# Output scatters of the last layer, issued behind the gathers of a later slot

## The chip, the cores and the metric

One core of one Trainium2 chip runs the whole computation in one launch. The metric is the device time of that launch in microseconds (us). Before the change three runs gave 2300.34, 2286.70 and 2286.37 us; the median is 2286.7 us.

## The reference

Sixteen graphs share one adjacency of 1024 nodes (about 8 edges in a row of 1024), with 128 features for each node. Four layers follow each other: three graph transformers (L0, L2, L3) and one graph attention layer (L1). The last one, L3, is what the change touches:

```python
Q, K, V = (h @ Wq), (h @ Wk), (h @ Wv)          # 8 heads of 16
scores = where(adj == 0, -inf, Q K^T / sqrt(16))
attn_out = softmax(scores) @ V
x = layer_norm(h + attn_out @ Wo + bo)
x = layer_norm(x + relu(x @ W1 + b1) @ W2 + b2)
```

The returned array holds x of L3 for every graph and node.

## The kernel before

**The sparse way.** Only the edges are computed. Nodes are sorted by degree and handled in blocks of 128 destinations. For each layer a table in DRAM holds one row of keys and values for each node; for a group of 8 graphs a row of an attention layer has 2048 floats (8 KB). A block's edges are packed in chunks: a chunk is 128 edge slots, one for each partition, and one indirect DMA on POOL's queue (`gathered`, L942) fetches the 128 table rows of a chunk, 1 MB if no slot is empty.

**Units, parts, slots.** A unit is one block of one group in one layer (2 groups of 8 blocks in each layer, 64 units). A unit's chunks are taken two at a time, and one more chunk (called MIX) is taken alone; each of these is a part. Most units have five parts, in the order pair, pair, pair, MIX, pair; block 0 has six and block 7 four. I call them p0, p1, p2, MIX, p3. The loop of the schedule (L1152) makes one pass for each part; a pass is a slot. In slot i VectorE (DVE) multiplies the gathered keys by the queries (`products`, L954), sums over a head (`exponentials`, L977), and weights the values of the part before (`weighted(i - 1)`, L1005). ScalarE (ACT) takes the exponent between these two; TensorE (PE) adds the weighted rows to their destinations (L1021).

**Gathers.** There are four buffers `e` (`EDGES = 4`). When `weighted(i - 1)` has read its buffer, L1195 refills it: `gathered(i - 1 + AHEAD)` with `AHEAD = 4`, so that slot i fetches the part of slot i + 3. In a five-part unit slot 0 fetches this unit's MIX, slot 1 its p3, and slots 2, 3 and 4 fetch p0, p1 and p2 of the next unit.

**Tails.** When a unit's sums are complete, `divided` (L1058, L1061) divides them in slot 1 of the next unit and leaves two tails (`attention_tail`), one for each half h of the group's 8 graphs. A tail is a generator of 13 steps: output projection, layer norm, feed-forward, layer norm, and in the last layer `finish` (L655), which turns the result back into rows (`outs`), yields twice and sends them to the output with an indirect scatter on POOL's queue (L676): 128 rows of 2 KB, 256 KB. A pacer (`others`, L1095) spreads 11 steps over the following slots. What is left is run at once when the next `divided` comes up, again in slot 1, behind that slot's gathers:

```python
                gathered(i - 1 + AHEAD)
                for _ in sizes:
                    pass
            if closing is not None and here:
                while any(gen not in free for gen in tails):
                    advance(tails)
```

With 11 paced steps out of 13, both scatters of a unit (h0 and h1) fall into this last stretch. The tile framework places the waits: an instruction that writes a tensor waits for those before it that wrote the same tensor. Each engine runs its instructions in the order in which the program issues them. The other instruction on POOL is the small sum `seen` (L1073), which `sizes` issues behind the gathers of slot 2.

So POOL's order in a five-part unit of the last layer is: MIX | p3, p3, scatter h0, scatter h1 | p0, p0, seen | p1, p1 | p2, p2, where a bar ends a slot. SyncE's queue (SP) loads the next block's features (L871) and copies a few query rows for MIX (L918).

Of the kernel before, what the change touches and what calls it, by code (L numbers as in the profile page):

```python
# [44 lines left out]
GR = 2  # L45
G = B // GR
HF = 2
# [90 lines left out]
def sparse_path(ctx: ExitStack, tc: tile.TileContext, a: dict, out: bass.AP, flag):  # L138


    nc = tc.nc
# [42 lines left out]
    places = const.tile([P, GR, HF, T], I32, name="places")  # L184
# [17 lines left out]
    def gather_buffer():  # L202
        return gathers.tile([P, max(4 * ROW, J * (ROW + G))], F32, tag="e", name="e")
# [434 lines left out]
    def turned(z, dst, gain=None, shift=None, dve=False):  # L638

        ps = bank([P, GH, P])  # L640
        for i in range(GH):
            nc.tensor.transpose(ps[:, i, :], z[:, i, :], ident)  # L642
        if dve and gain is None:
            nc.vector.tensor_copy(dst, ps)
        elif dve:
            nc.vector.tensor_scalar(dst, ps, gain, shift, ALU.mult, ALU.add)
        elif gain is None:
            nc.scalar.copy(dst, ps)  # L648
        else:
            nc.scalar.activation(dst, ps, AF.Identity, bias=shift, scale=gain)  # L650
# [4 lines left out]
    def finish(l, g, t, h, z, gain, shift, dve=False):  # L655
        if l + 1 < len(LAYERS):

            wanted[0] = True
            while held[0]:
                advance(slow)  # L660
            wanted[0] = False
            busy[0] += 1
            xn = states.tile([P, GH, P], F32, tag="xT", name="xT")
            turned(z, xn, gain, shift)
            yield "free"
            yield from project(l + 1, g, t, h, xn)
            busy[0] -= 1
            return
        xn = states.tile([P, GH, P], F32, tag="xT", name="xT")
        turned(z, xn, gain, shift, dve)  # L670
        yield
        o = twos.tile([P, GH, D], F32, tag="kv", name="outs")
        turned(xn, o, dve=dve)
        yield
        yield
        nc.gpsimd.indirect_dma_start(  # L676
            out=out.rearrange("n (k c) -> (n k) c", k=GR * HF),
            out_offset=bass.IndirectOffsetOnAxis(ap=places[:, g, h, t : t + 1], axis=0),
            in_=o.rearrange("p g d -> p (g d)"), in_offset=None,
        )  # L680

    def hidden():
        return ones_.tile([P, F * GH * P], F32, tag="f1", name="f1")
# [142 lines left out]
    units = [(l, g, t) for l in range(len(LAYERS)) for g in range(GR) for t in range(T)]  # L826
# [10 lines left out]
    def is_attention(u):  # L837
        return LAYERS[units[u][0]][1] is ATTN
# [86 lines left out]
    def gathered(i):  # L925
        if i >= len(parts):
            return
        u, pieces = parts[i]
        if u == T:
            while slow:  # L930
                while busy[0] and not held[0]:
                    advance(tails)
                advance(slow)
        l, g, t = units[u]
        width = tables[l, g].shape[1]
        many = 2 if is_attention(u) else J
        e = gather_buffer()
        es[i] = e[:, : many * width].rearrange("p (k c) -> p k c", k=many)
        for k, (j, r) in enumerate(sum(pieces, [])):
            if j == MIX:  # L940
                j, r = SHARED[t][0], COUNT[t][SHARED[t][0]]
            nc.gpsimd.indirect_dma_start(  # L942
                out=es[i][:, k, :], out_offset=None, in_=tables[l, g][:, :],
                in_offset=bass.IndirectOffsetOnAxis(
                    ap=idx[:, min(l, 1), t, j, r : r + 1], axis=0
                ),
                bounds_check=N - 1, oob_is_err=False,
            )
# [124 lines left out]
        nc.gpsimd.tensor_tensor(seen[:, :, :n], seen[:, :, :n], both, ALU.add)  # L1073

    tails = []
    fronts = []
    loads = []
    slow = []
# [3 lines left out]
    def advance(gens):  # L1082
        for gen in list(gens):
            got = next(gen, "end")
            if got == "end":
                gens.remove(gen)
            elif got == "free":
                free.append(gen)
# [23 lines left out]
    with tc.manual_schedule():  # L1112
        wide = [gather_buffer() for _ in range(EDGES)]
        setup, entry, weights = graph(wide), at_once(0), load_weights("L0")
        next(setup)
        next(weights)
        next(entry)
        more = [weights, load_graph_weights()]
        rest = slots()
        for i, room in enumerate(setup):  # L1120
            if i == T:
                for gen in more:
                    next(gen)
            if room == "load":
                for _ in loaded(0):
                    next(entry, None)
            elif room == "queries":
                for _ in entry:
                    pass
                for _ in queries(0):  # L1130
                    pass
            elif isinstance(room, str):
                next(rest)
            else:
                for _ in range(room):
                    next(entry, None)
        for _ in entry:
            pass
        scratch.close()
        prods = ctx.enter_context(tc.tile_pool(name="prods", bufs=4))  # L1140
        smalls = ctx.enter_context(tc.tile_pool(name="smalls", bufs=3))
        slow.append(at_leisure(1))
        second = loaded(1)
        next(second)
        for i in range(AHEAD - 1):
            gathered(i)
        nc.gpsimd.memset(wide[3], 0.0)
        gathered(AHEAD - 1)
        fronts.extend([islice(rest, 4), second] + more)
        closing, sizes = None, ()  # L1150
        begun = 0
        for i in range(len(parts) + 2):  # L1152
            here = i < len(parts)
            u = parts[i][0] if here else len(units)
            if here:
                l = units[u][0]
                if i and parts[i - 1][0] != u:
                    begun = i
                    if u < T - 1:
                        fronts.append(islice(rest, 4))  # L1160
                    if l + 1 < len(LAYERS) and LAYERS[l + 1][1] is ATTN:
                        if units[u][1:] == (0, 1):
                            more = load_weights(LAYERS[l + 1][0])
                            next(more)
                            next(more)
                        if units[u][1:] == (0, 4):
                            fronts.append(more)
                if is_attention(u):
                    products(i)
            if i > 1:  # L1170
                summed(i - 2)
                done = parts[i - 2][0]
                if parts[i - 1 : i] == [] or parts[i - 1][0] != done:
                    closing = divided(done)
                    next(closing)
            others()
            if here:
                exponentials(i)
            if here and i == begun + 1:
                if is_attention(u):  # L1180
                    shared(u)
                while loads:
                    advance(loads)
                if u + 1 < len(units):
                    fronts.append(queries(u + 1))
                loads.append(loaded(u + 2))
                if u:
                    advance(loads)
            others()
            if 0 < i <= len(parts):  # L1190
                weighted(i - 1, 0)
                if not is_attention(parts[i - 1][0]):
                    others()
                    weighted(i - 1, 2)
                gathered(i - 1 + AHEAD)  # L1195
                for _ in sizes:
                    pass
            if closing is not None and here:
                while any(gen not in free for gen in tails):
                    advance(tails)  # L1200
                next(closing)
                sizes, closing = closing, None
                passes = 3 if is_attention(u) else 4
                steps = STEPS if is_attention(done) else GRAPH_STEPS
                steps -= LATE[units[done][0]]
                pace[:] = 0.0, steps / (passes * sum(part[0] == u for part in parts) - 1)
            others()
            if i + 1 >= len(parts) or parts[i + 1][0] != u:

                while fronts:  # L1210
                    advance(fronts)
        while tails:
            advance(tails)
        for _ in closing:
            pass
        while tails:
            advance(tails)
# [435 lines left out]
```

## Time and profile before

The profiled execution is told by its span, from the first to the last instruction.

| | before |
|---|---|
| runs: median (lowest to highest) | 2286.7 us (2286.37 to 2300.34) |
| span of the profiled execution | 2290.8 us, 36572 instructions |
| mean granted TensorE clock | 0.956 |
| PE / DVE / ACT / POOL busy | 90% / 82% / 67% / 46% |
| gathers L942 | 576, mean 1466 ns of POOL each |
| scatters L676 | 32, median 2112 ns of POOL each, from 1735.9 to 2286.2 us |
| DMA | 636 MB, mean 278 GB/s; 59.3% of the engines' time for POOL's queue, 18.9% for SP's |

POOL's busy time is what it takes to issue a DMA; the transfer itself runs on the 16 DMA engines. A wait in POOL's queue is listed as idle time ahead of the instruction that waited, with the engine that released it; where several semaphores were waited for, the engine named is the one that came last by the records. The stretch from 1733.0 to 2224.5 us (13 units of the last layer, from one `divided` to another) is the one to look at; in it DVE is busy 417.9 of 491.5 us, PE 440.3, ACT 344.7, POOL 231.9, and the DMA engines 73%.

### The profile page before, as it was taken

Reading aid. Unit: us, or ns where it says so; the run is one execution under the profiler, and the core shown is the slowest. Engines: PE = TensorE matmul, PEld = TensorE weight load, DVE = VectorE, ACT = ScalarE, POOL = GpSimd, SP = SyncE. Lnnn points to the kernel's source line nnn. Section 1 sums busy time; section 2 is a strip of 40 time slices with the busy share of each in tenths; the row PEclk is TensorE's granted clock in tenths of the full one; section 3 lists DMA queues with packets and bytes.
Section 4 is the critical chain, followed back from the end, with each engine's and each line's share of the span. In section 5 each row is a group of like instructions: output and inputs, shape, how many; then the busy total and the mean of one; then the engine's idle time right before and its main releaser. Section 6 shows DMA issues by size and latency. Waiting matters only on the chain. (4 is left out here: it accounts for less than half of the span.)

```text
span 2290.8 us, 36572 instructions
## 1 busy us (share of the span) xinstructions
PE 2052.0 (90%) x13140; PEld 1271.6 (56%) x13140; DVE 1871.1 (82%) x1472; ACT 1530.3 (67%) x5041; POOL 1050.7 (46%) x730
## 2 busy tenths in 40 slices
PE   6479999899998999998899989999999988998987
PEld 5336666555555555554465655655655555555544
DVE  7898888588888477777988889988888887988783
ACT  3237777777776565556677777777777766776765
POOL 3355344245445278884443434333344444444540
PEclk8789999999999999999999999999999998999999
DMA  7868888678887699997998978888887877677750
GB/s 249 278 217 300 304 279 305 240 247 302 285 295 265 197 330 354 354 373 288 326 318 292 319 254 306 296 314 295 281 282 277 291 258 250 242 275 270 260 217 20
DMA packets 165197, 636.06 MB, mean 278 GB/s; under 512 B 35064, under 2 KB 37880, under 8 KB 116510
## 3 DMA queue, kind: packets, MB, share of 16 engines
q0 software_dynamic: 89216, 485.08, 59.3%
q1 hardware_dynamic: 75792, 148.57, 18.9%
q8 instruction: 105, 1.72, 0.3%
q14 instruction: 84, 0.69, 0.1%
HBM read 581.08 MB, written 92.34 MB: 294 GB/s over the span
## 5 line engine op out<-in xcount | busy, mean ns | idle before, releaser
L942 POOL DMA_INDIRECT e<-table,idx x576 | 844.2, 1466 | 1022.1 <-DVE pr L1005 796.6
L1005 DVE TENSOR_TENSOR pr<-e,ex 128x2048 f32<-128x2048 f32 (+1 forms) x320 | 661.3, 2075 | 55.9 <-ACT ex L981 32.7
L954 DVE TENSOR_TENSOR pr<-e,qr 128x2048 f32<-128x2048 f32 x192 | 439.7, 2290 | 160.3 <-DMA e<-table,idx 91.5
L1021 PE MATMUL acc<-pr,marks 128*32 128x512 f32 x2624 | 528.5, 616 | 20.3 <-DVE pr L1005 16.4
L977 DVE TENSOR_REDUCE sc<-pr 128x128 f32<-128x2048 f32 (+1 forms) x240 | 497.5, 2073 | 8.0
L620 ACT ACTIVATE z<-yps,root 128x128 f32<-128x128 f32 x888 | 319.0, 390 | 35.6 <-PE yps L735 16.8
L1021 PEld LDWEIGHTS acc<-pr,marks 128*32 128x32 f32 x2624 | 108.7, 111 | 280.9 <-issue 231.6
L635 ACT ACTIVATE z<-yps,rstd 128x128 f32<-128x128 f32 x888 | 255.0, 371 | 7.2
L731 PE MATMUL yps<-W,f 128*128 128x128 f32 x1520 | 252.6, 283 | 7.7 <-ACT f L726 1.9
L726 ACT ACTIVATE f<-ps,b 128x512 f32<-128x512 f32 x190 | 130.6, 695 | 160.4 <-PE ps L717 159.7
L731 PEld LDWEIGHTS yps<-W,f 128*128 128x128 f32 x1520 | 205.7, 193 | 51.7 <-issue 26.2
L572 PE MATMUL ps<-Wkv,xT 128*128 128x256 f32 x768 | 212.2, 417 | 20.0 <-ACT xT L648 14.4
L908 ACT COPY qr<-ps 128x512 f32<-128x512 f32 x384 | 197.1, 602 | 47.7 <-PE ps L905 47.7
L642 PE MATMUL ps<-ident,z 128*128 128x128 f32 x896 | 179.7, 300 | 41.4 <-ACT z L635 36.6
L642 PEld LDWEIGHTS ps<-ident,z 128*128 128x128 f32 x896 | 116.2, 143 | 167.7 <-ACT z L635 86.5
L717 PE MATMUL ps<-x,W 128*128 128x512 f32 x384 | 193.9, 630 | 12.5 <-ACT x L650 12.4
L620 ACT ACTIVATION_READ_ACCUMULATOR z<-yps,root 128x1 f32 x888 | 203.7, 229 | 0.0
L905 PE MATMUL ps<-q,rep 32*128 32x512 f32 x768 | 166.5, 661 | 36.4 <-ACT q L900 34.0
L572 PEld LDWEIGHTS ps<-Wkv,xT 128*128 128x128 f32 x768 | 146.5, 204 | 73.9 <-ACT qr L908 18.0
L981 ACT ACTIVATE ex<-sc 128x128 f32<-128x128 f32 (+1 forms) x240 | 76.4, 318 | 157.9 <-DVE sc L977 157.8
L576 ACT COPY kv<-ps 128x512 f32<-128x512 f32 x176 | 103.3, 593 | 108.1 <-PE ps L572 85.8
L706 PE MATMUL yps<-Wo,oT 128*128 128x128 f32 x768 | 159.9, 291 | 10.0 <-ACT oT L648 10.0
(174 smaller groups left out, 2724.2 us busy)
## 6 DMA issues: line engine op xcount, KB each, us to landing
table<-kv SPq DMA_DIRECT2D x88, 512.0 KB
kept<-xT SPq DMA_DIRECT2D x96, 256.0 KB
x<-kept SPq DMA_DIRECT2D x48, 512.0 KB
qx<-qr SPq DMA_DIRECT2D x48, 256.0 KB
e<-table,idx POOLq DMA_INDIRECT x576
table<-kv SPq DMA_DIRECT2D x32, 256.0 KB
qx<-qr SPq DMA_DIRECT2D x18, 384.0 KB
qx<-qr SPq DMA_DIRECT2D x42, 128.0 KB
```

The source lines that it names most:

```text
L572: nc.tensor.matmul(ps[:, k, :], x[:, i + k, :], w[LAYERS[l][0], "Wkv"], start=True, stop=True,)
L620: nc.scalar.activation(z[:, i, :], y[:, i, :], AF.Square, scale=D**-0.5, bias=root, accum_out=total[:, i : i + 1],)
L635: nc.scalar.activation(z[:, i, :], y[:, i, :], AF.Copy, scale=rstd[:, i : i + 1])
L642: nc.tensor.transpose(ps[:, i, :], z[:, i, :], ident)
L717: nc.tensor.matmul(ps, p["W1"][:, f * P : (f + 1) * P], x1.rearrange("p g n -> p (g n)"), start=True, stop=True,)
L731: nc.tensor.matmul(ps[:, i, :], f1[:, f, i * P : (i + 1) * P], p["W2"][:, f, :], start=(f == 0), stop=False,)
L908: nc.scalar.copy(qs[u][:, j, h * GH * D : (h + 1) * GH * D], pss[j])
L942: nc.gpsimd.indirect_dma_start(out=es[i][:, k, :], out_offset=None, in_=tables[l, g][:, :], in_offset=bass.IndirectOffsetOnAxis(ap=idx[:, ...
L954: nc.vector.tensor_tensor(prs[i][0][:, :n, :], es[i][:, :n, :ROW], qx[u].rearrange("p (o c) -> p o c", o=1) if (MIX, 0) in piece else of_p ...
L977: nc.vector.tensor_reduce(sc[:, :n, :], prs[i][0][:, :n, :].rearrange("p k (a d) -> p k a d", d=HD), mybir.AxisListType.X, ALU.add,)
L1005: nc.vector.tensor_tensor(prs[i][k0 // 2][:, :m, :].rearrange("p k (a d) -> p k a d", d=d), es[i][:, k0 : k0 + m, base : base + ROW].rearr ...
L1021: nc.tensor.matmul(outs[32 * j : 32 * j + 32], marks[:, mark, :], rhss, start=(chunk == mine[0]), stop=(chunk == mine[-1]),)
```

## The change

In the last layer `finish` no longer issues its scatter. It puts a closure on a list, `scatters`; only the very last unit's scatters are still issued where they were. The loop issues the closures behind a slot's gathers, but only those that were on the list when the slot before reached the same point:

```diff
+        def scatter():
+            nc.gpsimd.indirect_dma_start(
+                out=out.rearrange("n (k c) -> (n k) c", k=GR * HF),
+                out_offset=bass.IndirectOffsetOnAxis(ap=places[:, g, h, t : t + 1], axis=0),
+                in_=o.rearrange("p g d -> p (g d)"), in_offset=None,
+            )
+
+        if (l, g, t) == units[-1]:
+            scatter()
+        else:
+            scatters.append(scatter)
...
-        closing, sizes = None, ()
+        closing, sizes, ready = None, (), []
...
                 gathered(i - 1 + AHEAD)
+                for scatter in ready:
+                    scatter()
+                ready = scatters[:]
+                scatters.clear()
                 for _ in sizes:
                     pass
...
         while tails:
             advance(tails)
+        for scatter in ready + scatters:
+            scatter()
         for _ in closing:
             pass
```

A closure that is made in slot 1 behind the gathers is moved to `ready` in slot 2 and issued in slot 3. The instructions themselves and their number stay as they are.

More of the change, by code (lines that the diff above doesn't have):

```diff
@@ L675, in finish @@
         yield
[L676 to L680, printed above, removed]
+        def scatter():
[8 more added lines that the diff above has]
+            scatters.append(scatter)
     def hidden():
@@ L1075, in sparse_path @@
     tails = []
+    scatters = []
     fronts = []
```

## The prediction

> **What bounds the kernel now.** The chain that ended last covers under 1% of the span, so it says nothing on the middle. I went to DVE's waits in the stretch of the last layer in which scatters are issued (1733 to 2230 us):
>
> ```profile
> DVE pr L954 <- DMA e<-table,idx: 61.9, 13, 5.9
> DVE pr L954 <- PE acc L1021: 4.2, 3, 1.9
> ```
>
> DVE waits 61.9 us for gathered rows. The same view for 1180 to 1690 us (layer 2, no scatters) has 9.6 us of this, so it belongs to the scatters' layer. DVE's order of time shows where:
>
> ```profile
> 2088.19 2.29 DVE L977 TENSOR_REDUCE sc<-pr 128x128 f32<-128x2048 f32 x1
> 2090.40 1.22 DVE L1005 TENSOR_TENSOR pr<-e,ex 128x1024 f32<-128x1024 f32 x1
> 2097.07 2.29 DVE L954 TENSOR_TENSOR pr<-e,qr 128x2048 f32<-128x2048 f32 x1 [5.46 <-DMA e<-table,idx]
> ```
>
> It is once a unit, at slot 0: p0 is late. Twelve such waits of 3.70 to 5.88 us sum to 61.7 us: eleven in ordinary (five-part) units, 56.7 us, mean 5.16; one of 4.98 us at the four-part unit near 1950 us; none at the six-part unit after it. Why p0 is late, in POOL's order of time:
>
> ```profile
> 2066.34 2.80 POOL L942 DMA_INDIRECT e<-table,idx  x1 [7.33 <-DVE pr L1005]
> 2073.06 0.99 POOL L942 DMA_INDIRECT e<-table,idx  x1 [3.92 <-DVE pr L1005]
> 2074.36 0.99 POOL L942 DMA_INDIRECT e<-table,idx  x1 [0.30 <-issue]
> 2075.65 2.11 POOL L676 DMA_INDIRECT out<-outs,places  x1 [0.30 <-ACT qr L908]
> 2084.50 2.32 POOL L676 DMA_INDIRECT out<-outs,places  x1 [6.74 <-ACT rstd L627]
> 2087.12 1.95 POOL L942 DMA_INDIRECT e<-table,idx  x1 [0.31 <-ACT z L620]
> 2089.38 1.01 POOL L942 DMA_INDIRECT e<-table,idx  x1 [0.31 <-issue]
> 2090.41 1.51 POOL L1073 TENSOR_TENSOR seen<-seen,both 128x128 f32<-128x128 f32 x1
> 2092.07 1.00 POOL L942 DMA_INDIRECT e<-table,idx  x1 [0.16 <-issue]
> ```
>
> Row by row: MIX; p3 twice; scatter h0; scatter h1 after 6.74 us of idle; p0 twice; seen; p1. DVE released p0's buffer at 2081.3 (end of L1005 of slot 2), but its first gather starts at 2087.12. The engine named for h1's wait, ACT, is not it: h0 waits for nothing and h1's rows were written just before h0's. The query on the scatter line shows the wait itself, from 2073.9, fetched ahead:
>
> ```profile
> L676 POOLq EVENT_SEMAPHORE  x1: 9877/9877/9877, 2073.9 to 2073.9; - x1
> ```
>
> It ends at 2083.74. In the trace's landing records the semaphore that h0 increments gets its sixteenth mark at 2083.71. So h1 waits until h0's 256 KB have landed: both write `out`. And h0 lands behind p3 (second gather landed 2083.04).
>
> **What the Trainium skill says.** "DMA: Bandwidth & Descriptors", section "Two DMAs through the same engine are not ordered": order comes only from the issuing engine's wait for the first DMA's completion semaphore; the trace has that wait. Same page, "SWDGE vs HWDGE vs iDMA": DMAs issued from GpSimd have one queue; the trace agrees, h0 lands 0.67 us behind p3. Same page, "Anatomy of one DMA": about 2.0 us plus bytes/436e3, an estimate of 2.6 us for a scatter alone; at the end of the trace, with empty queues, h0 starts at 2282.70, takes 0.99, and h1 starts 2.5 us later. "SBUF — State Buffer", "Who interferes with whom": a DVE instruction with two SBUF inputs blocks a GpSimd one that reads SBUF. MIX agrees: 2.80 us instead of 0.99, ending 0.9 us after DVE's L954 (2065.99 + 2.28).
>
> **The change, part by part.** No instruction is added or removed. Both closures are made in slot 1 behind p3's gathers, go to `ready` in slot 2 and are issued in slot 3. POOL's order becomes MIX | p3 p3 | p0 p0 seen | p1 p1 h0 h1 | p2 p2. SP's queue isn't moved past anything. h0's rows are long done; but h1 still waits for h0 to land, and now p2 is queued behind it. The stall isn't removed, it goes two slots on. I cost it as a timetable in an ordinary unit, zero at slot 2's L954, DVE durations from the trace: slot 2 takes 6.72, slot 3 4.59, slot 4 5.74 (these three from 2074.57 to 2091.62), next slot 0 6.73, slot 1 with `divided` 8.58; sum 32.36.
>
> Before, by this count: p3's buffer is free at the end of slot 1's L1005, 2072.79; p0's second gather ends at 2090.39 and DVE goes on at 2097.07: 24.3 us. To p0's use there are 18.8 us of DVE work. 24.3 - 18.8 = 5.5, the wait seen.
>
> After:
> - p0: buffer free at 6.80; gathers 7.07-8.84 (blocked until 7.94) and 9.15-10.15; seen to 11.7.
> - p1: free at 11.39; 11.9-14.5 (L954 until 13.60, + 0.9) and 14.8-15.8. Then h0 16.1-17.95 (blocked until 17.05).
> - Landings. In the unit where SP's row loads ran beside them, gathers from 1783.32 landed at 1791.30, 1793.83, 1796.30, 1798.79: the first 8.0 us after its start, then one every 2.5. So p0 lands at 17.6, p1 at 22.6, h0 at 23.2. p0 was due at 17.05: a wait of 0.6, new. p1 is due at 24.4: no wait.
> - h1 starts 0.8 after that landing (2083.71 to 2084.50), at 24.0, about where DVE's next L954 begins (24.4). If it gets in first: h1 to 25.4, p2 25.7-27.6 and 27.9-28.9. If not: h1 to 27.6, p2 27.9-28.9 and 29.2-32.1.
> - p2 lands 6.6 after its second gather (2090.39 to 2096.95), at 35.5; in the second case 4.4 after it, as the first one is through by then (4.4 is 2089.07 to 2093.49), at 36.5. Due 32.96. Wait 2.5 to 3.5, up to 5.7 if 6.6 holds there too.
>
> Together 3.1 to 6.3 us a unit; I take 4.0, since most of the interval above belongs to one doubtful term. Eleven units: 11 x (5.16 - 4.0) = 12.8 gained. Four-part unit: behind the scatters comes the next unit's MIX, one chunk due three slots (21 us) on, so of 4.98 about 0.5 stays: 4.5 gained. Six-part unit: p1 of the next unit is behind them, due 19.2 us on against a chain of about 25; PE held DVE up there before (3.2 us ahead of L1058), so I take 3 lost. Sum: 14.3 us. The last two units keep their order and POOL is idle there: 0, both ways. Span 2290.8 - 14.3 = 2276.5. The span lies 4.1 above the median; taking that off, 2272.
>
> The cover: what hides h1's wait is POOL's own idle time ahead of MIX (7.33 us in slot 0). Without it the whole wait would fall on p2.
>
> **The rivals.**
> - *The stall is absorbed.* p2 arrives in time and DVE becomes the bound at 32.4 us a unit. All of 61.7 us gone gives 2225; with 1 us a unit for PE, 2237. For it: available time grows from 18.8 to 21.0 us, and PE is idle waiting for ACT's z, 28.6 us in this stretch. Against: h1's wait has the same cause and now has four gathers ahead of h0 in the queue instead of two.
> - *Slower: h0 lands late in a fuller queue.* In layer 2, p1's second gather landed 11.5 and 13.9 us after its issue ended (1601.27 to 1612.81; 1712.26 to 1726.15); I use 6.8. With 11.5, h0, h1 and p2 move 4.7 us on: 8.7 a unit, 11 x (8.7 - 5.16) = 39 us lost, less the 1.5 gained at the two odd units: 2324. It decides from 1.2 us later than I take. Against: layer 2 also writes tables and kept rows; its DMA share is 86 to 91% of an ordinary unit, here 67 to 79%.
> - *Another wait takes its place.* Layer 2's units take 34.7 to 37.6 us with PE hardly idle (0.35 of 34.7 us in the shortest). If PE needs as much here, units stay near 37 whatever POOL does: 2280 to 2290. Against: the last layer has no projections for a next one (16 matmul records, 5 us a unit, against 8 short transposes more).
> - *The change doesn't do what it says*: "one slot" is two by my count of `ready`; were it one, h0 and h1 would stand behind p0, and p1 would be late instead: from the end of slot 2's L1005 (6.80) to its use (23.78) there are 17.0 us, so 24.3 - 17.0 = 7.3 us a unit, 11 x 2.1 = 24 us slower: 2310.
>
> **How the numbers follow.** Forecast (stall moves, shrinks a little; 2258 to 2290): 0.58. Absorbed: 0.17. Fuller queue: 0.12. Another wait: 0.11. One slot only: 0.02. The time is the forecast's, 2272. About 1% (22.9 us) can be told from no change: faster than 2263.8 is all of the second case and a sixth of the first, 0.26; slower than 2309.6 is most of the third and half of the last, 0.11; the rest 0.63. The range takes the upper end of the first case, half of the second's width and the start of the third: 2240 to 2305.
>
> **What would show it.** POOL's order with h0 and h1 between p1 and p2; an idle of 5 to 7 us ahead of h1 as before; DVE's wait for `e` at slot 2 (right behind `divided`) instead of slot 0, 2.5 to 4 us, and one of about 0.6 at slot 0. It is wrong if h1 starts without waiting for h0's landing, if no unit waits for `e` over 1 us, or if the waits are named PE.

## The result and the profile after

Thirteen runs of each kernel were compared. The changed kernel takes 2297.3 us (median), the one before 2291.1 us in the same comparison; the ratio is 1.0036, 95% interval 1.0013 to 1.0060. It is slower by a third of a per cent (8 us by the ratio, 6 by the medians), where 14 us of gain were forecast.

The two profiled spans, 2313.0 and 2290.8 us, differ by 22 us, but 12 of these are there before the stretch with the scatters begins, in a part where both kernels issue the same instructions. So I compare the stretch alone, 13 units from one `divided` to another. It takes 491.5 us before and 498.7 us after: 7.2 us more. The last unit then loses 3.0 us more to a late p2. Both together, 10 us, lie inside the interval of the runs (3 to 14 us). In the changed file the lines have moved: the gather is L949, the product L961, the weighting L1012, `divided` L1065 and L1068, the scatter L678.

POOL's order of time, after, in one unit (start, duration, what, and in brackets the idle time ahead):

```profile
2101.45 1.73 POOL L949 DMA_INDIRECT e<-table,idx  x1 [8.13 <-DVE pr L1012]
2103.49 0.99 POOL L949 DMA_INDIRECT e<-table,idx  x1 [0.30 <-issue]
2104.51 1.62 POOL L1080 TENSOR_TENSOR seen<-seen,both 128x128 f32<-128x128 f32 x1
2106.28 1.01 POOL L949 DMA_INDIRECT e<-table,idx  x1 [0.15 <-issue]
2107.60 2.00 POOL L949 DMA_INDIRECT e<-table,idx  x1 [0.30 <-issue]
2109.90 1.04 POOL L678 DMA_INDIRECT out<-outs,places  x1 [0.30 <-issue]
2121.96 3.00 POOL L678 DMA_INDIRECT out<-outs,places  x1 [11.02 <-DMA out<-outs,places]
2125.26 1.04 POOL L949 DMA_INDIRECT e<-table,idx  x1 [0.30 <-issue]
2126.60 2.90 POOL L949 DMA_INDIRECT e<-table,idx  x1 [0.31 <-issue]
```

The order is the one forecast: p0 twice, seen, p1 twice, h0, h1, p2 twice. h1 still waits, and this time the view names the releaser rightly: h0's own DMA. The wait has grown, from 6.2 to 8.6 us in the mean of the 13 units (11.0 in the one shown): h0 now stands behind four gathers instead of two. DVE's order of time in the same place:

```profile
2094.37 2.29 DVE L961 TENSOR_TENSOR pr<-e,qr 128x2048 f32<-128x2048 f32 x1 [2.65 <-DMA e<-table,idx]
...
2106.44 2.29 DVE L961 TENSOR_TENSOR pr<-e,qr 128x2048 f32<-128x2048 f32 x1 [0.63 <-PE acc L1028]
...
2115.08 2.29 DVE L961 TENSOR_TENSOR pr<-e,qr 128x2048 f32<-128x2048 f32 x1 [2.90 <-DMA e<-table,idx]
...
2134.53 2.29 DVE L961 TENSOR_TENSOR pr<-e,qr 128x2048 f32<-128x2048 f32 x1 [4.05 <-DMA e<-table,idx]
```

One wait of 5.5 us has become two. At 2094.37 and 2134.53, in slot 2 right behind `divided`, p2 is late: that is the stall that moved. At 2115.08, in slot 0, p0 is late, though POOL issued it as soon as its buffer was free. Over the eleven ordinary units the slot 2 waits average 2.65 us and the slot 0 waits 2.48: 5.13 us a unit, against 5.16 before. DVE's waits in the stretch say the same:

```profile
DVE pr L961 <- DMA e<-table,idx: 59.9, 22, 4.8
DVE pr L961 <- PE acc L1028: 6.2, 5, 2.3
```

59.9 us, plus the 3.0 in the last unit, stand against 61.9 before: the same sum in almost twice as many pieces (22 and one, against 13).

Why is p0 late? SP's queue, before and after, beside it:

```profile
2082.57 1.15 SPq L918 DMA_DIRECT2D qx<-qr  x2
2083.76 0.63 SPq L871 DMA_DIRECT2D x<-kept  x1
```

```profile
2102.39 1.14 SPq L925 DMA_DIRECT2D qx<-qr  x2
2104.58 0.33 SPq L878 DMA_DIRECT2D x<-kept  x1
```

SP issues its copies of query rows (2 x 256 KB) and a block's features (512 KB) when DVE has done MIX's product, in slot 3, in both kernels. Before, p0 was held until 2087.12, and by 2088.56 the landing records show all of SP's loads through; p0 landed 6.6 us after its last gather was issued. After, p0 starts at 2101.45, SP's 1 MB one microsecond later, and p0 lands 10.5 us after its last issue. In the mean of the eleven ordinary units it is 6.8 us before and 10.1 after. The Trainium skill, "DMA: Bandwidth & Descriptors", section "Queues, rings and completion order", says that each DMA engine takes turns between the queues that have work for it; the later landing agrees. By this reading the late start of p0 had kept the two apart; the experiments test it.

### The profile page after: what moved, and what is told of

Same layout as the page of the kernel before. It is cut to its first block, busy times and chain, and to the rows that moved or that the text cites. A ratio compares the mean times of both kernels' runs of the same rounds, so it can differ in the third digit from the quotient of the medians.

```text
span 2313.0 us, 36584 instructions
## 1 busy us (share of the span) xinstructions
PE 2070.5 (90%) x13140; PEld 1283.9 (56%) x13140; DVE 1877.0 (81%) x1472; ACT 1528.3 (66%) x5041; POOL 1061.6 (46%) x730
## 5 line engine op out<-in xcount | busy, mean ns | idle before, releaser
L949 POOL DMA_INDIRECT e<-table,idx x576 | 860.6, 1494 | 999.8 <-DVE pr L1012 767.4
L1012 DVE TENSOR_TENSOR pr<-e,ex 128x2048 f32<-128x2048 f32 (+1 forms) x320 | 661.5, 2076 | 52.0 <-ACT ex L988 27.8
L961 DVE TENSOR_TENSOR pr<-e,qr 128x2048 f32<-128x2048 f32 x192 | 441.1, 2297 | 170.7 <-DMA e<-table,idx 97.6
L572 PE MATMUL ps<-Wkv,xT 128*128 128x256 f32 x768 | 207.1, 409 | 18.6 <-ACT xT L648 12.4
L912 PE MATMUL ps<-q,rep 32*128 32x512 f32 x768 | 177.9, 678 | 51.0 <-ACT q L907 37.0
L724 PE MATMUL ps<-x,W 128*128 128x512 f32 x384 | 193.3, 628 | 12.4 <-ACT x L650 12.3
L713 PE MATMUL yps<-Wo,oT 128*128 128x128 f32 x768 | 165.8, 300 | 8.1 <-ACT oT L648 7.5
```

The source lines that it names most:

```text
L572: nc.tensor.matmul(ps[:, k, :], x[:, i + k, :], w[LAYERS[l][0], "Wkv"], start=True, stop=True,)
L724: nc.tensor.matmul(ps, p["W1"][:, f * P : (f + 1) * P], x1.rearrange("p g n -> p (g n)"), start=True, stop=True,)
L949: nc.gpsimd.indirect_dma_start(out=es[i][:, k, :], out_offset=None, in_=tables[l, g][:, :], in_offset=bass.IndirectOffsetOnAxis(ap=idx[:, ...
L961: nc.vector.tensor_tensor(prs[i][0][:, :n, :], es[i][:, :n, :ROW], qx[u].rearrange("p (o c) -> p o c", o=1) if (MIX, 0) in piece else of_p ...
L1012: nc.vector.tensor_tensor(prs[i][k0 // 2][:, :m, :].rearrange("p k (a d) -> p k a d", d=d), es[i][:, k0 : k0 + m, base : base + ROW].rearr ...
```

## The experiments

My theory had two parts. *One*: h1's wait for h0's landing is the stall, and the change only moved it. *Two*: p0, once on time, loads beside SP's rows. Rivals were the scatters' own transfers, p0's own queue behind it, and the place of the same bytes not mattering. All ratios are to the kernel before, run beside them; "stretch" is the same 13 units in the profile (491.5 before, 498.7 changed). "Slot 0" sums DVE's waits for p0 in these units (61.7 before, 28.9 changed): every wait over 0.3 us at slot 0's product that ended within 0.6 us of a gather's landing. The view of waits puts some of these down to PE or "issue", so its lines for `e` can fall short.

| kernel | ratio (95% interval) | stretch, us | slot 0, us |
|---|---|---|---|
| before, h1 to another tensor | 0.9937 (0.9913-0.9960) | 476.8 | 40.1 |
| changed, h1 to another tensor | 0.9905 (0.9874-0.9936) | 464.7 | 27.2 |
| before, one scatter for both halves | 0.9944 (0.9917-0.9970) | 477.7 | 41.2 |
| changed, one scatter for both halves | 0.9910 (0.9885-0.9934) | 469.6 | 27.5 |
| one scatter a slot | 0.9896 (0.9852-0.9940) | 468.3 | 30.0 |
| both in slot 2 | 1.0189 (1.0156-1.0223) | 535.9 | 22.2 |
| changed, no feature loads | 0.9960 (0.9942-0.9977) | 484.2 | 16.8 |
| one a slot, no feature loads | 0.9839 (0.9806-0.9872) | 458.6 | 20.3 |
| one a slot, no loads, no copies | 0.9767 (0.9742-0.9792) | 433.3 | none |
| one a slot, features by ACT | 0.9846 (0.9810-0.9882) | 458.2 | 18.2 |
| one a slot, features and copies by ACT | 0.9858 (0.9824-0.9893) | 452.8 | none |
| before, features and copies by ACT | 0.9994 (0.9980-1.0008) | 488.0 | 22.6 |

**Without h1's wait.** The edit, in the kernel before and in the changed one (`other` is a DRAM tensor of the output's shape, so half of the output is left out):

```diff
-                out=out.rearrange("n (k c) -> (n k) c", k=GR * HF),
+                out=(other if h else out).rearrange("n (k c) -> (n k) c", k=GR * HF),
```

> The kernel before, but the second half's scatter (h1) writes another DRAM tensor, so half of the output is left out and h1 need not wait for h0 to land; it takes as many rows as before from the same queue. Theory 1 (POOL's stall is h1's wait for h0's landing): the idle of some 6.5 us ahead of h1 goes, p0 is issued at once, and DVE's waits for e in the last 13 units fall from 62 us to under 35 us (what is left is p0 loading beside SP's row loads, 2 to 3 us a unit): 25 to 50 us faster than before. Rival (it is the scatters' own transfers and issue time that hold the gathers up): waits stay over 50 us and the time stays within 10 us of before.

> The changed kernel with h1's scatter going to another DRAM tensor (half of the output is left out). Theory 1: the idle of 9 to 11 us ahead of h1 goes, p2 is in time, and DVE's wait at slot 2 (about 2.6 us a unit, 30 us in all) goes; the wait at slot 0 (about 2.7 us) stays: 25 to 35 us faster than the changed kernel, and about as fast as the kernel before with the same edit. Rival (scatter transfers, not the wait): within 10 us of the changed kernel.

The same rows leave on the same queue. DVE's waits for `e` in the stretch, the kernel before first:

```profile
DVE pr L955 <- DMA e<-table,idx: 34.3, 9, 5.0
```

```profile
DVE pr L962 <- DMA e<-table,idx: 27.2, 11, 3.7
```

In the kernel before, h1's idle time is gone, and the waits for `e` fall from 61.9 to 34.3 us. But two waits at slot 0 (5.7 us) are named PE and "issue" although p0 lands 0.1 and 0.5 us before they end; with these 40.1 us are left, more than the 35 that I set, and the time falls by 0.63% (14 us), less than the 25 us that I set as the least. So h1's wait accounts for a third of the stall alone: without it p0 is issued on time and is still 3.6 us late in an ordinary unit, which theory two has to explain. In the changed kernel 27.2 us are left, all at slot 0, no wait is left in slot 2, and the ratio, 0.9905 against 1.0036, makes it 30 us faster, as expected. The scatters' transfers are not what makes p2 late there.

**One scatter instead of two.** A unit's halves are put in one tile and sent with 4 KB rows:

```diff
...
+        elif h:
+            nc.gpsimd.indirect_dma_start(
+                out=out.rearrange("n (k c) -> (n k) c", k=GR),
+                out_offset=bass.IndirectOffsetOnAxis(ap=pairs[:, g, t : t + 1], axis=0),
+                in_=both_halves[g, t].rearrange("p h g d -> p (h g d)"), in_offset=None,
+            )
...
```

> The whole computation. Both halves of a unit's output are put side by side and sent by one scatter of 128 rows of 4 KB where h1's scatter stood in the kernel before; there is no second scatter to wait. Theory 1: no idle ahead of it, waits for e under 35 us, 25 to 50 us faster than before. Rival (the transfer of 512 KB itself is what the gathers wait for): within 10 us of before.

> The whole computation. The change with one scatter of 4 KB rows for both halves of a unit, issued behind p1: no second scatter that could wait. Theory 1: the slot 2 wait goes, slot 0's of 2 to 3 us stays: 20 to 30 us faster than the changed kernel, about as fast as one scatter a slot. Rival (512 KB in one go delay p2's transfer as much as the wait did): within 10 us of the changed kernel.

At h1's old place it gives 0.9944, as much as sending h1 elsewhere did and again less than I set, with 41.2 us left at slot 0; in the changed place 0.9910, some 29 us below the changed kernel, as expected, with no wait in slot 2. With no second scatter there is nothing to wait for, and the whole output is written.

**The place of the wait.** One scatter a slot puts h0 behind p1 and h1 behind p2:

```diff
-                for scatter in ready:
-                    scatter()
-                ready = scatters[:]
+                if ready:
+                    ready.pop(0)()
+                ready = ready + scatters
                 scatters.clear()
```

"Both in slot 2" issues both closures one slot earlier than the change does, behind p0:

```diff
-                for scatter in ready:
+                for scatter in scatters:
                     scatter()
-                ready = scatters[:]
                 scatters.clear()
```

> The whole computation. As changed, but at most one scatter is issued in a slot: h0 behind p1 (slot 3), h1 behind p2 (slot 4). h1 still waits for h0, but only MIX is queued behind it, and MIX has three slots (20 us) until its use. Theory 1: the slot 2 wait goes, the slot 0 wait stays: 20 to 35 us faster than the changed kernel, 15 to 30 faster than before. Rival (h1's wait only moves on once more and makes MIX or p3 late): waits for e stay near 60 us, time within 10 us of the changed kernel.

> The whole computation. Both scatters go behind the gathers of the next slot, slot 2, behind p0 and ahead of p1 (the change delays them to slot 3). Theory 1: h1's wait then holds p1 up, which has only 17.0 us to its use against 18.8 (before) and 21.0 (changed): a wait of 5 to 8 us a unit at slot 1, 5 to 30 us slower than the changed kernel. Rival (the place does not matter): within 5 us of the changed kernel.

Both came out as theory one has it, the second a little beyond: 1.0189 is 35 us above the changed kernel. Its waits for `e`, in the stretch:

```profile
DVE pr L961 <- DMA e<-table,idx: 84.8, 22, 7.1
```

They grow to 84.8 us. In the eleven ordinary units p1 is late by 5.5 to 7.1 us, 6.1 in the mean (7.3 was worked out), and p0 by 2.0. With one scatter a slot POOL's order of time is:

```profile
2080.86 1.88 POOL L678 DMA_INDIRECT out<-outs,places  x1 [0.30 <-issue]
2083.05 1.02 POOL L949 DMA_INDIRECT e<-table,idx  x1 [0.30 <-issue]
2084.37 0.99 POOL L949 DMA_INDIRECT e<-table,idx  x1 [0.31 <-issue]
2091.69 3.01 POOL L678 DMA_INDIRECT out<-outs,places  x1 [6.33 <-DMA out<-outs,places]
2095.01 1.02 POOL L949 DMA_INDIRECT e<-table,idx  x1 [0.30 <-issue]
```

h1 still waits 6.3 us here, but behind it stands MIX (2095.01), which lands at 2099.16 and is used at 2106.81. The wait is still there and costs nothing. What is left is p0 at slot 0: 30.0 us, of which the view puts only 15.1 down to `e`. (In the other five units it names PE, but p0 lands 0.12 us before the product there too.)

**SP's loads.** The features are left out by letting a block use those of its group's first block, the copies likewise; or both are kept and issued from ACT's queue, at their place in the program:

```diff
+        if l == len(LAYERS) - 1 and t:
+            xs[units[u]] = xs[l, g, 0]
+            return
...
-        nc.sync.dma_start(
+        (nc.scalar if l == len(LAYERS) - 1 else nc.sync).dma_start(
```

> The changed kernel in which the last layer's blocks do not load their own features from DRAM (512 KB a unit on SyncE's queue left out; a block uses those of the first block of its group, so the values are others). Theory 2 (p0 is late at slot 0 because it now loads beside SP's row loads, which before were through by then): p0's landing after its issue falls from 10.5 us to about 8.5, the wait at slot 0 from 2.7 us to under 1.3; the slot 2 wait stays at 2 to 3: 12 to 25 us faster than the changed kernel. Rival (p0 is late because p1 and h0 are queued right behind it on POOL's own queue and share the engines): the slot 0 wait stays over 2 us, less than 8 us gained.

> The kernel with one scatter a slot (h0 behind p1, h1 behind p2), without the last layer's feature loads as in the run above. Theory 2: both waits go; DVE waits for e under 12 us in the last 13 units and units come down to 33 to 34 us: 15 to 30 us faster than one scatter a slot with the loads, near 2245. Rival as above: within 8 us of it.

> The whole computation. One scatter a slot, and in the last layer the features are loaded from ACT's queue instead of SP's, where they stand behind the copies of query rows that wait for MIX's product. They then start in slot 1 or 2 by the program's order, earlier than p0's gathers, beside p3. Theory 2: p0 lands 1.5 to 2 us sooner, slot 0's wait falls to about 1 us: 10 to 25 us faster than one scatter a slot. Rival: the same bytes in the same unit cost the same wherever they stand, within 8 us of it.

> One scatter a slot, without the last layer's feature loads and now also without its copies of query rows for MIX (about 256 KB each, two or three a unit, on SyncE's queue; a block uses those of the first block, so the values are others). Leaving out the feature loads alone took p0's landing from about 10.3 to 9.2 us after its last issue and left waits of about 2 us at slot 0. Theory 2 (what is left is the copies, which start 1 us after p0's first gather): landing at 7.5 us or less, DVE's waits for e in the last layer under 10 us, 8 to 15 us faster than without the feature loads alone. Rival (p0 is late for its own queue's sake, p1 behind it): within 5 us of that run.

> The whole computation. One scatter a slot, and in the last layer both the feature loads and the copies of query rows are issued from ACT's queue at their place in the program (slot 1), not from SP's, which runs them as soon as the buffer is free, 1 us after p0's first gather. Theory 2: nothing collides with p0 any more; slot 0 waits under 1 us; 5 to 15 us faster than with the feature loads alone on ACT's queue. Rival: the waits move to p3 or to MIX's product, which then waits for its query rows, or ACT is held up: no faster than that run.

> The whole computation. The kernel before, scatters where they were, with the last layer's feature loads and copies on ACT's queue. Theory 1 and 2 together: p0 is late by h1's wait, and by then SP's loads are through, so moving them gains little: within 12 us of before, waits for e over 45 us. Rival (the loads are the whole trouble and h1's wait is not needed to explain it): 25 us or more faster than before.

Without the features the changed kernel gains 17 us (0.9960 against 1.0036), p0's landing goes from 10.1 to 9.3 us after its issue (mean of the ordinary units; I had set 8.5), and the slot 0 wait from 2.48 to 1.4 us (set: under 1.3): half the bytes, some 40% of the wait. With one scatter a slot the same edit takes the slot 0 waits from 30.0 to 20.3 us where I set under 12, and gains 13 us where I set 15 or more. So something was left, and leaving out the copies too showed what. DVE's waits in the stretch then:

```profile
DVE pr L968 <- PE acc L1035: 5.1, 12, 1.6
DVE pr L1019 <- ACT ex L995: 3.3, 1, 3.3
```

No wait for `e` at all; p0 lands 6.6 us after its issue, as before the change (6.8), and an ordinary unit takes 32.64 us against the 32.36 of DVE's own work. Theory two holds for the features and for the copies, and the rival (p0's own queue) falls, since p1 stands behind p0 as in the other runs.

Keeping the loads but moving the features to ACT's queue gives the lowest ratio of the versions that compute everything: 0.9846, 35 us below the kernel before, stretch 458.2 us against 468.3. (Its interval overlaps that of one scatter a slot.) The slot 0 wait goes from 2.7 to 1.7 us a unit, where I set about 1. Its waits:

```profile
DVE pr L961 <- DMA e<-table,idx: 16.3, 10, 2.9
DVE pr L961 <- PE acc L1028: 8.3, 6, 1.6
```

Moving the copies as well clears the waits for `e`: p0 lands 6.9 us after its issue, with nothing left out, against 10.1 with one scatter a slot. So it is the moment of these loads that makes p0 late, and not only their bytes. But I had set 5 to 15 us of gain, and the rival came true: MIX's product now waits for its query rows in some units (5.0 us in two waits, the longest 4.0), 13.4 us of waits are named PE, and the whole is no faster (0.9858; the intervals overlap).

The kernel before with the same two moves takes as long as without them, 0.9994, as expected; but its waits are not those that I expected (over 45 us for `e`):

```profile
DVE pr L955 <- PE acc L1022: 21.3, 9, 4.1
DVE pr L955 <- DMA e<-table,idx: 14.4, 8, 5.3
DVE pr L955 <- issue: 10.7, 4, 3.4
```

h1's wait is still there (7.7 us in the mean), and p0's landing still ends 22.6 us of waits at slot 0. But 30 us of waits for PE and "issue" have come up in slot 4, ahead of it, and cover part of p0's lateness. So that the loads don't matter as long as h1's wait holds p0 back fits this run but isn't shown by it: a gain there could have been lost again on ACT's queue, and why PE is late here was not tested.

## Why the prediction was wrong, step by step

- *Where the stall is and why* (h1 waits for h0's landing; p0 is behind it): right as to the wait, but it is not the whole stall. Sending h1 to another tensor removed the wait and left 40.1 of 61.7 us at slot 0.
- *What the change moves* (two slots, to between p1 and p2; p2 late at slot 2): right, in order and in place. The idle time ahead of h1 was set at 5 to 7 us and measured 8.6 in the mean.
- *The slot 0 wait*, "0.6, new": this is the step that failed. It measured 2.48 us. The forecast's 4.0 us a unit was this 0.6 and so 3.4 at slot 2; measured are 2.48 and 2.65, together 5.13. Over eleven units the slot 0 term was 21 us too good and the slot 2 term 8 us too bad, so that 12.4 of the 12.8 us of gain forecast there did not come. The term behind it is "the first 8.0 us after its start, then one every 2.5". I took it from a unit in which SP's loads had been issued before p0 and landed by 1787.84, before p0's first landing at 1791.30. "SP's queue isn't moved past anything" is true, but p0 was moved to where SP's loads start. In the changed kernel they start one microsecond after p0's first gather and compete with all of it: in the unit shown p0's second gather lands 20.6 us after slot 2's start, not 17.6, p1's at 26.7, not 22.6, and h0 at 27.3, not 23.2.
- *The slot 2 wait*, 2.5 to 3.5 us: 2.65, but by luck. In the unit shown p2 landed at 40.1 (35.5 to 36.5 forecast) and was due at 36.1 (32.96 forecast): p0's lateness put off both, and the two errors cancelled.
- *The odd units*: 4.5 gained and 3 lost by count; measured, the waits for `e` there go from 4.98 to 1.69 + 4.76, so 1.5 lost instead of 1.5 gained.
- *The rivals*: the fuller queue was the nearest one. It named h0's late landing, and 27.3 against 23.2 is most of the 4.7 us it assumed, but by SP's loads, not by a slower queue; and its 2324 counted that landing in full although the due time moved with it. The one-slot price, 7.3 us, was near (6.1 measured), but the total was not: "both in slot 2" is 43 us slower than the kernel before, against 24 worked out, since p0 is late there too and 13.8 us of waits for PE were not counted. That PE would take DVE's place is shown false by the run at 32.64 us a unit, though narrowly: PE is busy 32.0 us of such a unit there.
- *A scatter alone*, 2.6 us by estimate: the last mark of h0's landing at the end of the trace comes 2.7 us after its start. The 2.5 us that the prediction sets beside it are counted from the end of h0's issue.

The profile of the kernel before already had the second cause, in layer 2, where no scatter holds p0 back:

```profile
1447.05 1.73 POOL L942 DMA_INDIRECT e<-table,idx  x1 [6.29 <-DVE pr L1005]
1448.18 1.54 SPq L918 DMA_DIRECT2D qx<-qr  x2
1461.23 2.29 DVE L954 TENSOR_TENSOR pr<-e,qr 128x2048 f32<-128x2048 f32 x1 [3.39 <-PE ps L717]
```

SP's loads start one microsecond after p0, p0 lands 11.0 us after its last issue, at 1461.11, and the product waits for it, though the view names PE. So the 9.6 us that the prediction read for layer 2 left such waits out. (A table was being written there as well, which is why the prediction set those landings aside.)

The rest of the 7.2 us: in the stretch itself the waits for `e` fall by 2.0 us, DVE's other waits (PE, ACT and "issue") grow by 6.0, and its busy time by 3.1 (417.9 to 421.0), of which 2.1 are told below. Why the other waits grow stays open. The granted clock of the stretch was 0.95 before and 0.93 after and PE was busy for 440.3 and 450.3 us; no run here separates this from the change.

## What to carry to other kernels

A wait that is moved goes with its instruction: ask what stands behind it at the new place and how much time that has until its use, and prefer the place with the most (here MIX, used three slots later). Then ask what the freed transfer will run into: a late transfer may have been keeping out of another queue's way, and a landing time may only be taken over from a unit in which the other queues' loads start at the same moment. Check the engine that a wait is named after against the landing records. Two writes to one tensor from one queue that wait for each other, as here, are best made one, or set a transfer apart.

## What the runs showed that I had not expected

POOL's sum `seen` also slows DVE. In the stretch, the products of 128x2048 take 2291 ns in the mean before and 2323 ns after (52 each). Seven of those after take 2539 to 2542 ns, and these are the seven that start while `seen` is still running on POOL:

```profile
1757.20 1.62 POOL L1080 TENSOR_TENSOR seen<-seen,both 128x128 f32<-128x128 f32 x1
1758.42 2.54 DVE L961 TENSOR_TENSOR pr<-e,qr 128x2048 f32<-128x2048 f32 x1
```

Before, one of the 52 starts so, and takes 2567 ns. It isn't the issuing of gathers: the 19 products after that start while POOL issues a gather or a scatter take 2279 to 2293 ns. In the changed kernel `seen` starts a microsecond into a weighting and often reaches into the next product. That weighting takes some 2321 instead of 2282 ns, in all 13 units; a gather's issue starts with it as well, so which of the two slows it is not shown. Together this is 2.1 us. The block between the two engines, which the prediction counted for POOL alone, works both ways.
